# Splitting the exponentials of a float32 attention product into two float32r halves

## The chip, the cores and the metric

The kernel runs on one core of one Trainium2 chip. The metric is the device time of one execution in microseconds; several executions are made and their median is quoted. The kernel before took 4827.44 us (median of 3 runs, 4765.34 to 4841.02). The runs of the kernel before scatter by 1.6%, and with their clock: 4765 us goes with a mean granted clock of 0.955, 4840 us with 0.930. "Faster" and "slower" are verdicts at 2%; a ratio whose interval lies across that mark is called unclear.

## The reference

Two attention layers over an image batch of 8 x 512 x 32 x 32. Layer 0 has 8 heads of 64 channels and quantises q, k and v to 8 bits ("fake quantisation"), so that they are integers times a scale. Layer 1 is one full-width attention and is not touched here.

```python
# layer 0, cut
h = group_norm(xf, gn_w, gn_b)
qkv = einsum('oc,bct->bot', qkv_w, h) + qkv_b[None, :, None]
q, k, v = split(qkv.reshape(b * 8, -1, T), 3, axis=1)      # T = 1024
q, k, v = fake_quant(q), fake_quant(k), fake_quant(v)      # (integer) * scale
w = einsum('bct,bcs->bts', q * scale, k * scale)
w = softmax(w, axis=-1)
a = einsum('bts,bcs->bct', w, v)                           # <- the product that changes
a = einsum('oc,bct->bot', proj_w, a) + proj_b
x = xf + a
```

## The kernel before

Each head takes eight steps, one per tile of 128 key tokens. A step computes the scores of those keys against all 1024 queries (`st`), takes their exponential (`pt`), and adds the product of the exponentials with the integer values (`av`). The row maxima that the *next* head needs are computed in between: scores the other way round (`sm`), reduced on VectorE (`negm`). The integers of q and k are held as bfloat16, in 64 rows; three more rows carry minus the row's maximum, in three bfloat16 parts.

```python
ps_s = tc.tile_pool(name="ps_s", bufs=2, space=PSUM)    # two slots, shared by st and sm
q_aug = [augp.tile([AUG, T], BF, ...) for i in range(2)]   # AUG = 64 + 3 rows
k_aug = [augp.tile([AUG, T], BF, ...) for i in range(2)]

def row_max(g, t):
    ps = big_ps(f"sm_{g}_{t}")
    for hf in range(NH):                                # two halves of 512 tokens
        nc.tensor.matmul(ps[:, bass.ts(hf, 512)],
            lhsT=q_aug[a][0:CH, bass.ts(t, P)], rhs=k_aug[a][0:CH, bass.ts(hf, 512)], ...)
    nc.vector.tensor_reduce(negm[g][:, t : t + 1], ps, AX.X, ALU.max, negate=True)
# [cut]
def step_av(s):
    pt = pts.pop(s)
    for hf in range(NH):
        nc.tensor.matmul(av[hf][0 : CH + 1, :], lhsT=vq[b][:, s, h, :],
            rhs=pt[:, bass.ts(hf, 512)], start=(s == 0), stop=(s == NT - 1))

for s in range(NT):
    ps = big_ps(f"st_{g}_{s}")
    for hf in range(NH):
        nc.tensor.matmul(ps[:, bass.ts(hf, 512)],
            lhsT=k_aug[a][:, bass.ts(s, P)], rhs=q_aug[a][:, bass.ts(hf, 512)], ...)
    pts[s] = ptp.tile([P, T], F32, tag="p", ...)
    nc.scalar.activation(pts[s], ps, AF.Exp, scale=esc)
    if nxt is not None:
        row_max(nxt, s)
    if s > 0:
        step_av(s - 1)
step_av(NT - 1)
if nxt is not None:
    put_max(nxt)                                        # maxima into rows 64:67 of q_aug
# [cut: sums, reciprocal, output]
```

## Time and profile before

| | before |
|---|---|
| median time | 4827.44 us |
| TensorE / VectorE / ScalarE busy | 93% / 37% / 23% |
| attention of layer 0, one image | 240.7 us |
| one steady step of a head | 2.79 us |
| one head, not the first of an image (mean) | 30.75 us |

The prediction below shows the busy times, the chain, the groups and the step. Three further lines of the kernel before matter for what follows. From its page: the row of the granted TensorE clock over 40 equal slices, in tenths of full speed, and the group of the score product (count, busy us and mean ns of one, idle time before and what ended it).

```profile
PEclk9999998999988998899889998999899988998899
...
L357 PE MATMUL st<-q_aug,k_aug 67*128 67x512 bf16 x1024 | 350.6, 418 | 53.5 <-DVE q_aug L312 44.0
```

The attention of image 6 as a stretch (busy time and instruction count of TensorE, its weight loads, VectorE, ScalarE and GpSimd, then granted clock, DMA share, GB/s).

```profile
3314.15:3554.90 240.75, 217.62 (x576) 57.11 (x575) 116.41 (x155) 95.48 (x93) 9.08 (x7) 0.86 0.09 29
```

The clock is at 0.9 or 0.8 nearly everywhere. Inside attention it averages 0.86: it drops at each change of heads, when TensorE waits, and is back after 3.4 us in the shortest heads (28.2 us) and after up to 17.1 us in the longest (34.1 us).

### The profile page before, as it was taken

Reading aid. Unit: us, or ns where it says so; the run is one execution under the profiler, and the core shown is the slowest. Engines: PE = TensorE matmul, PEld = TensorE weight load, DVE = VectorE, ACT = ScalarE, POOL = GpSimd, SP = SyncE. Lnnn points to the kernel's source line nnn. Section 1 sums busy time; section 2 is a strip of 40 time slices with the busy share of each in tenths; the row PEclk is TensorE's granted clock in tenths of the full one; section 3 lists DMA queues with packets and bytes.
Section 4 is the critical chain, followed back from the end, with each engine's and each line's share of the span. In section 5 each row is a group of like instructions: output and inputs, shape, how many; then the busy total and the mean of one; then the engine's idle time right before and its main releaser. Section 6 shows DMA issues by size and latency. Waiting matters only on the chain.

```text
span 4828.6 us, 28560 instructions
## 1 busy us (share of the span) xinstructions
PE 4482.2 (93%) x11328; PEld 1704.1 (35%) x11328; DVE 1781.7 (37%) x2618; ACT 1120.7 (23%) x1217; POOL 108.8 (2%) x102
## 2 busy tenths in 40 slices
PE   7999897889988998999989999999999988998999
PEld 3444442234322442244224422343234322442244
DVE  4544445541245114511442234323442245124311
ACT  0000002421243114311341133213321233124211
POOL 0000000000000000000000000000000000000000
PEclk9999998999988998899889998999899988998899
DMA  4222212010101000100100000001000101000000
GB/s 178 96 90 89 79 74 87 18 31 0 40 18 31 0 35 18 31 4 9 40 18 22 9 35 18 27 0 44 18 27 0 40 18 31 0 35 14 1 0 18
DMA packets 69830, 162.31 MB, mean 34 GB/s; under 512 B 23232, under 2 KB 23232, under 8 KB 69056
## 3 DMA queue, kind: packets, MB, share of 16 engines
q1 hardware_dynamic: 64176, 135.31, 8.0%
q10 hardware_dynamic: 5520, 25.17, 1.4%
q8 instruction: 89, 1.46, 0.1%
q14 instruction: 45, 0.37, 0.0%
HBM read 92.82 MB, written 67.11 MB: 33 GB/s over the span
## 4 chain that ended last, share of the span: by engine, by line
PE 85%; DVE 7%; issue 3%; ACT 2%; DMA 2%; POOL 0%; SPq 0%; POOLq 0%; ACTq 0%; DVEq 0%
PE av L346 19%; PE qk L417 9%; PE o L478 9%; PE s L444 9%; PE pj L394 9%; PE qkps L172 8%; PE sm L285 6%; PE st L357 5%; PE v2ps L431 5%; PE vps L190 4%; DVE negm L292 3%; PE tp L470 1%; DVE q_aug L312 1%; DMA x<-in_x_dram 1%; ACT pt L365 1%
## 5 line engine op out<-in xcount | busy, mean ns | idle before, releaser
L346 PE MATMUL av<-pt,vq 128*65 128x512 f32 x2048 | 1126.9, 678 | 70.6 <-ACT pt L365 70.6
L292 DVE TENSOR_REDUCE negm<-sm 128x1 f32<-128x1024 f32 x512 | 626.0, 1224 | 891.9 <-PE sm L285 891.1
L365 ACT ACTIVATE pt<-st,esc 128x1024 f32<-128x1024 f32 x512 | 569.9, 1113 | 1003.2 <-PE st L357 1003.2
L346 PEld LDWEIGHTS av<-pt,vq 128*65 128x65 f32 x2048 | 298.9, 152 | 602.0 <-issue 420.2
L172 PE MATMUL qkps<-h,wqkv 128*128 128x512 f32 x1024 | 462.4, 615 | 30.7 <-ACT h L123 30.4
L417 PE MATMUL qk<-h,wres 128*128 128x512 f32 x1024 | 457.8, 610 | 29.6 <-ACT h L123 29.6
L444 PE MATMUL s<-k,q 128*128 128x512 f32 x1024 | 443.4, 592 | 0.0
L478 PE MATMUL o<-pT,v 128*128 128x512 f32 x1024 | 442.9, 593 | 0.3 <-DVE pT L472 0.3
L285 PE MATMUL sm<-k_aug,q_aug 64*128 64x512 bf16 x1024 | 348.1, 424 | 59.3 <-DVE negm L292 32.3
L357 PE MATMUL st<-q_aug,k_aug 67*128 67x512 bf16 x1024 | 350.6, 418 | 53.5 <-DVE q_aug L312 44.0
L402 DVE SCALAR_TENSOR_TENSOR x<-pj,vec,x 128x512 f32<-128x512 f32 x128 | 95.3, 750 | 643.3 <-PE pj L394 641.6
L172 PEld LDWEIGHTS qkps<-h,wqkv 128*128 128x128 f32 x1024 | 201.6, 198 | 285.6 <-issue 252.8
L417 PEld LDWEIGHTS qk<-h,wres 128*128 128x128 f32 x1024 | 200.4, 197 | 281.1 <-issue 250.8
L478 PEld LDWEIGHTS o<-pT,v 128*128 128x128 f32 x1024 | 193.9, 190 | 244.5 <-issue 241.1
L438 DVE TENSOR_TENSOR v<-v2ps,vb 128x512 f32<-128x512 f32 x64 | 44.2, 691 | 632.2 <-PE v2ps L431 632.2
L444 PEld LDWEIGHTS s<-k,q 128*128 128x128 f32 x1024 | 193.3, 190 | 237.2 <-issue 237.2
L285 PEld LDWEIGHTS <-q_aug 64*128 64x128 bf16 x1024 | 64.7, 96 | 523.2 <-issue 427.2
L123 ACT ACTIVATE h<-h,vec 128x1024 f32<-128x1024 f32 x64 | 68.3, 1137 | 750.7 <-DVE h L119 750.7
L394 PE MATMUL pj<-q,wres 128*128 128x512 f32 x512 | 222.3, 592 | 0.0
L394 PE MATMUL pj<-ao,wres 128*128 128x512 f32 x512 | 221.8, 594 | 0.0
L431 PE MATMUL v2ps<-wres,h 128*128 128x512 f32 x512 | 221.0, 592 | 0.0
L190 PE MATMUL vps<-wqkv,h 128*128 128x512 f32 x512 | 221.0, 592 | 0.0
(108 smaller groups left out, 2315.3 us busy)
## 6 DMA issues: line engine op xcount, KB each, us to landing
qk_d<-qk SPq DMA_DIRECT2D x64, 512.0 KB, 2.6
rqk<-qk_d SPq DMA_DIRECT2D x64, 512.0 KB, 3.7
x<-in_x_dram SPq DMA_DIRECT2D x32, 512.0 KB, 6.3
v_d<-v SPq DMA_DIRECT2D x64, 256.0 KB, 2.0
x<-in_x_dram ACTq DMA_DIRECT2D x8, 2048.0 KB, 7.9
rv<-v_d SPq DMA_DIRECT2D x32, 512.0 KB, 4.2
out_dram<-x SPq DMA_DIRECT2D x16, 1024.0 KB, 4.2
wres<-in_w_res_dram ACTq DMA_DIRECT2D x5, 1024.0 KB, 9.7
```

The source lines that it names most:

```text
L172: nc.tensor.matmul(ps[:, bass.ts(hf, 512)], lhsT=wqkv[:, cc, h * 3 * CH : h * 3 * CH + 2 * CH], rhs=hn[:, cc, bass.ts(hf, 512)], start=(cc ...
L190: nc.tensor.matmul(ps, lhsT=hn[:, cc, bass.ts(t, P)], rhs=wv_cols[:, cc, :, 2, :], start=(cc == 0), stop=(cc == CC - 1),)
L285: nc.tensor.matmul(ps[:, bass.ts(hf, 512)], lhsT=q_aug[a][0:CH, bass.ts(t, P)], rhs=k_aug[a][0:CH, bass.ts(hf, 512)], start=True, stop=True,)
L292: nc.vector.tensor_reduce(negm[g][:, t : t + 1], ps, AX.X, ALU.max, negate=True)
L346: nc.tensor.matmul(av[hf][0 : CH + 1, :], lhsT=vq[b][:, s, h, :], rhs=pt[:, bass.ts(hf, 512)], start=(s == 0), stop=(s == NT - 1),)
L357: nc.tensor.matmul(ps[:, bass.ts(hf, 512)], lhsT=k_aug[a][:, bass.ts(s, P)], rhs=q_aug[a][:, bass.ts(hf, 512)], start=True, stop=True,)
L365: nc.scalar.activation(pts[s], ps, AF.Exp, scale=esc)
L394: nc.tensor.matmul(ps, lhsT=wres[:, w, cc, bass.ts(oc, P)], rhs=src[:, cc, :], start=(cc == 0), stop=(cc == CC - 1),)
L417: nc.tensor.matmul(ps[:, bass.ts(hf, 512)], lhsT=wres[:, w, cc, bass.ts(oc, P)], rhs=hn[:, cc, bass.ts(hf, 512)], start=(cc == 0), stop=(c ...
L431: nc.tensor.matmul(ps, lhsT=hn[:, cc, bass.ts(t, P)], rhs=wres[:, WV1, cc, :], start=(cc == 0), stop=(cc == CC - 1),)
L444: nc.tensor.matmul(ps[:, bass.ts(hf, 512)], lhsT=qt[:, cc, bass.ts(n, P)], rhs=kt[:, cc, bass.ts(hf, 512)], start=(cc == 0), stop=(cc == C ...
L478: nc.tensor.matmul(ps, lhsT=vt[:, m, bass.ts(dc, P)], rhs=pT[:, m, :], start=(m == 0), stop=(m == NT - 1),)
```

## The change

One float32 product is replaced by two cheaper ones. The exponential is taken once into float32 and once into a float32r tile (`hi`; float32r is a four-byte type, as the diff shows where it reads such tiles as float32, and the change assumes that it keeps fewer bits than float32); VectorE computes what is missing (`lo = pt - hi`); and the values, being integers, go into a float32r tile too. In the kernel before a float32 product of 512 columns takes 858 ns (64 instructions, two a product, in 27.47 us) and a bfloat16 product about 0.22 us (`st`, 0.45 us for two): four passes against one, as passes are counted here. Each half should take one pass too; this was my estimate, as the kernel before has no float32r product. The intent is to halve the `av` work, at the price of a second exponential and a subtraction on engines that were under 40% busy. Comments were dropped from the file as well, which changes nothing.

```diff
+F32R = mybir.dt.float32r
+    php = ctx.enter_context(tc.tile_pool(name="php", bufs=2))
-        vq[b] = act.tile([P, NT, HEADS, CH + 1], F32, tag="v", name=f"vq_{b}")
-        nc.gpsimd.memset(vq[b][:, :, :, CH : CH + 1], 1.0)
+        vq[b] = act.tile([P, NT, HEADS, CH + 1], F32R, tag="v", name=f"vq_{b}")
+        nc.gpsimd.memset(vq[b][:, :, :, CH : CH + 1].bitcast(F32), 1.0)
         ...
         def step_av(s):
-            pt = pts.pop(s)
-            for hf in range(NH):
-                nc.tensor.matmul(... rhs=pt[:, bass.ts(hf, 512)],
-                    start=(s == 0), stop=(s == NT - 1))
+            for part, pt in enumerate(pts.pop(s)):
+                for hf in range(NH):
+                    nc.tensor.matmul(... rhs=pt[:, bass.ts(hf, 512)],
+                        start=(s == 0 and part == 0), stop=(s == NT - 1 and part == 1))
         ...
-            pts[s] = ptp.tile([P, T], F32, tag="p", name=f"pt_{g}_{s}")
-            nc.scalar.activation(pts[s], ps, AF.Exp, scale=esc)
+            pt = ptp.tile([P, T], F32, tag="p", name=f"pt_{g}_{s}")
+            nc.scalar.activation(pt, ps, AF.Exp, scale=esc)
+            hi = php.tile([P, T], F32R, tag="hi", name=f"hi_{g}_{s}")
+            nc.scalar.activation(hi, ps, AF.Exp, scale=esc)
+            lo = php.tile([P, T], F32R, tag="lo", name=f"lo_{g}_{s}")
+            nc.vector.tensor_sub(lo, pt, hi.bitcast(F32))
+            pts[s] = (hi, lo)
```

More of the change, by code (lines that the diff above doesn't have):

```diff
@@ L343, in step_av @@
         def step_av(s):
-            pt = pts.pop(s)
-            for hf in range(NH):
-                nc.tensor.matmul(
-                    av[hf][0 : CH + 1, :],
-                    lhsT=vq[b][:, s, h, :],
-                    rhs=pt[:, bass.ts(hf, 512)],
-                    start=(s == 0),
-                    stop=(s == NT - 1),
-                )
+            for part, pt in enumerate(pts.pop(s)):
+                for hf in range(NH):
+                    nc.tensor.matmul(
+                        av[hf][0 : CH + 1, :],
+                        lhsT=vq[b][:, s, h, :],
+                        rhs=pt[:, bass.ts(hf, 512)],
+                        start=(s == 0 and part == 0),
+                        stop=(s == NT - 1 and part == 1),
+                    )
         for s in range(NT):
```

## The prediction

> **What bounds the kernel now.** I read the page's busy times, the chain of waits by line, the groups, and then the timeline of one head in image 6. The page first: TensorE is busy 93% of the span, VectorE 37%, ScalarE 23%, and the chain that ends last is mostly TensorE, with the changed line (L346, `av`) as its largest part.
>
> ```profile
> PE 4482.2 (93%) x11328; PEld 1704.1 (35%) x11328; DVE 1781.7 (37%) x2618; ACT 1120.7 (23%) x1217; POOL 108.8 (2%) x102
> ...
> PE av L346 19%; PE qk L417 9%; PE o L478 9%; PE s L444 9%; PE pj L394 9%; PE qkps L172 8%; PE sm L285 6%; PE st L357 5%; PE v2ps L431 5%; PE vps L190 4%; DVE negm L292 3%; PE tp L470 1%; DVE q_aug L312 1%; DMA x<-in_x_dram 1%; ACT pt L365 1%
> ...
> L346 PE MATMUL av<-pt,vq 128*65 128x512 f32 x2048 | 1126.9, 678 | 70.6 <-ACT pt L365 70.6
> L292 DVE TENSOR_REDUCE negm<-sm 128x1 f32<-128x1024 f32 x512 | 626.0, 1224 | 891.9 <-PE sm L285 891.1
> L365 ACT ACTIVATE pt<-st,esc 128x1024 f32<-128x1024 f32 x512 | 569.9, 1113 | 1003.2 <-PE st L357 1003.2
> ```
>
> The kernel issues 1024 `av` products and the group counts 2048, so one float32 product is two instructions. A busy mean of 678 ns is not the pace, because ends are modelled: the chain has a float32 group of the same moving width with nothing between, 64 instructions in 27.47 us, so 429 ns each and 858 ns a product.
>
> ```profile
> 1148.48 27.47 PE s L444 x64
> ```
>
> Averages hide that the change touches attention of layer 0 only: from 3314.15 to 3554.88 us in image 6, 240.7 us, or 1926 us in eight images, 40% of the span. One steady step there (of eight per head):
>
> ```profile
> 3384.23 0.60 PE L285 MATMUL sm<-k_aug,q_aug 64*128 64x512 bf16 x2
> ...
> 3384.76 0.61 PE L357 MATMUL st<-q_aug,k_aug 67*128 67x512 bf16 x2
> 3384.87 1.23 DVE L292 TENSOR_REDUCE negm<-sm 128x1 f32<-128x1024 f32 x1 [1.66 <-PE sm L285]
> ...
> 3385.21 1.88 PE L346 MATMUL av<-pt,vq 128*65 128x512 f32 x4
> ...
> 3385.47 1.11 ACT L365 ACTIVATE pt<-st,esc 128x1024 f32<-128x1024 f32 x1 [1.68 <-PE st L357]
> ...
> 3387.02 0.60 PE L285 MATMUL sm<-k_aug,q_aug 64*128 64x512 bf16 x2
> ```
>
> Starts give the pace: `sm` 0.53, `st` 0.45, four `av` 1.81, together 2.79 us, with no gap on TensorE. VectorE and ScalarE each idle over 1.5 us of it. So a step is bound by TensorE. A head is not: mrow to mrow is 31.19 us (3398.35 to 3429.54), of which eight steps are 22.3. The rest is the change of heads:
>
> ```profile
> 3399.52 0.38 PE L357 MATMUL st<-q_aug,k_aug 67*128 67x512 bf16 x1 [0.56 <-DVE q_aug L312]
> ...
> 3400.59 1.11 ACT L365 ACTIVATE pt<-st,esc 128x1024 f32<-128x1024 f32 x1 [2.12 <-PE st L357]
> ...
> 3401.76 2.89 PE L346 MATMUL av<-pt,vq 128*65 128x512 f32 x4 [1.26 <-ACT pt L365]
> ...
> 3402.45 1.15 ACT L277 ACTIVATE q_aug<-qi,nmagic 64x1024 bf16<-64x1024 f32 x1 [0.74 <-DVE qi L266]
> ...
> 3404.82 1.01 PE L285 MATMUL sm<-k_aug,q_aug 64*128 64x512 bf16 x2 [0.17 <-ACT k_aug L278]
> ...
> 3406.89 1.11 ACT L365 ACTIVATE pt<-st,esc 128x1024 f32<-128x1024 f32 x1 [2.12 <-PE st L357]
> ```
>
> TensorE waits there for row maxima, exponentials and quantised q and k in turn, and afterwards runs at half clock, as the stretches show (busy times, then the granted clock in the third column from the end):
>
> ```profile
> 3384.00:3395.00 11.00, 11.00 (x33) 3.09 (x32) 4.90 (x4) 4.45 (x4) 0.00 (x0) 1.00 0.00 0
> ...
> 3402.00:3408.00 6.00, 5.49 (x10) 0.90 (x8) 2.55 (x3) 3.40 (x3) 1.30 (x1) 0.55 0.28 88
> ```
>
> [...]858 ns against about 0.22 us for a bfloat16 product (`st`, 0.45 for two).[...] The trace's nearest, L387 on 64 partitions, is 1213.
>
> **The change part by part.** *Removed from TensorE:* per step, four `av` instructions of 429 ns become two products in each of two halves, four instructions again, at one pass each. Taking the bfloat16 pace of 216 ns (my choice; no float32r is in this trace), 2048 x 213 ns = 436 us go. TensorE's step becomes 0.53 + 0.45 + 4 x 0.216 + 0.1 for switches = 1.94 us.
>
> *Added to ScalarE:* a second exponential of the same scores per step, 512 x 1.113 = 570 us. It also keeps the scores' PSUM slot longer.
>
> *Added to VectorE:* 512 subtractions of 128 x 1024 fp32 at about 1.22 us, 625 us. A step has 2.44 us of VectorE work with the maximum; a head 8 x 2.44 + some 5.5 us of small work = 25 us.
>
> *Moved:* `vq` is written as float32r, same instructions; `lo` must wait for both exponentials and for VectorE.
>
> So no engine alone is a bound above 2.79: TensorE 1.94, [...]VectorE 2.44. The path of waits is. A scores slot is held from the start of `st` (0.71 to the first exponential, as above: 3384.76 to 3385.47), through two exponentials (2.25), to release (0.06 seen between an activation's end and its waiter): 3.02 us, against 1.88 now. There are two slots for `st` and `sm` together, and `sm` holds one for 0.64 + 1.23 + 0.06 = 1.93. If `st` keeps coming back to its own slot, **a step takes 3.02 us**, slower than 2.79 although TensorE idles a third of it.
>
> Head: from the last exponential of a head to the second of the next is 13.05 us now (3393.84 to 3406.89), through `av`, copies, sums, then qi, q_aug, k_aug, `sm`, `st`. New: `av` ends later by the second exponential and the subtraction but is shorter by 1.1; I add 1.0 for VectorE's queue: 14.0. Six more steps: 18.1. Half-clock steps at about 3.5 cost 1.3 more. Sum 33.4 against 31.19, **+2.2 us**, for 56 heads +123 us; the first heads of images (23.4 us, few waits now) get 8 x 0.23 plus the longer tail, 3 us each, +24. Sum **+150 us**. Layer 1 and phase 1 don't move.
>
> **Rivals.** *A, TensorE still sets the pace:* then 436 us would go, 4390 us. For it: 93% busy, the chain 85% TensorE. Against: it needs steps of 1.94, below VectorE's 2.44. I give it next to nothing. *B, slots are traded:* `st` can take the slot that `sm` left. One line shows that it happens (a score product waiting for the row maximum just before it):
>
> ```profile
> 3324.44 0.59 PE L357 MATMUL st<-q_aug,k_aug 67*128 67x512 bf16 x2 [1.31 <-DVE negm L292]
> ```
>
> Then the bound is (3.02 + 1.93)/2 = 2.47, near VectorE's 2.44; really some 2.7, as subtractions delay maxima. That takes 0.3 x 6 x 64 = 115 us off: about 4860 to 4880, within 2%. *C, in-order queues lock:* TensorE runs `sm` before `av`, VectorE the subtraction before the maximum. Then two steps take 0.71 + 2.31 + 1.22 + 1.22 (maximum) + 0.12 + 0.53 + 0.97 = 7.0, or 3.5 a step, +185 us on top, about 5160. Now the trace has `st`, `av`, `sm`, which speaks against it. *D, the clock:* at 64% busy TensorE may stay at half rate; steps then take about 3.5, like C. Against: at half rate it would be nearly always busy[...].
>
> **Range and chances.** 4827 + 150 = 4977 by the middle path. C or D at about a third adds 60, B at a fourth takes 30: 5010, and as orders seldom come out ideal I say 5020 us. Range 4870 (B) to 5270 (C and D partly together). Runs of before scatter by 1.6%. Slower by over 2% (above 4924) 0.73, within 2% 0.21, faster 0.06: that needs steps under 2.5 and shorter changes of heads.
>
> **What would show it.** Right: `av` spaced 216 ns; PE busy down by over 400 us while the span grows; exponentials x1024 of 1.11 us; subtractions x512 near 1.22; steady steps at 3.0; `st` waiting for the second exponential; heads at 33 to 34 us; layer 1 unchanged at 264 us an image. Wrong: steps below 2.7 with `st` waiting for maxima (B), 3.5 (C), a low clock in steady steps (D), or a float32r product at more than one pass, which up to two passes would hardly change the time, since TensorE would still be under 2.9 a step.

## The result, and the profile after

The changed kernel took **5203.65 us** (median of 4 runs, 5201.69 to 5206.18), against 4833.65 us for the kernel before in the same session: a ratio of 1.0825, 95% interval 1.0724 to 1.0927. Ratios here and below are the mean time of one kernel's fast runs over that of the other's fast runs of the same rounds, so they are not quite the ratios of the medians.

So the change makes the kernel 8.25% slower, where the forecast of 5020 us meant 4%. The time lies inside the range, but for a reason that the prediction argued against: its middle path was 4977 us, and the room above came from rivals C and D, at about a third together. First the page of the changed kernel: busy times and the clock row, then groups.

```profile
PE 4629.4 (89%) x11328; PEld 1794.2 (35%) x11328; DVE 2391.4 (46%) x3130; ACT 1629.6 (31%) x1729; POOL 126.6 (2%) x102
...
PEclk9999985579856995699559965798569956995699
...
L370 ACT ACTIVATE pt<-st,esc 128x1024 f32<-128x1024 f32 x512 | 570.9, 1115 | 793.0 <-PE st L359 793.0
L348 PE MATMUL av<-hi,vq 128*65 128x512 f32 x1024 | 576.3, 660 | 127.8 <-ACT hi L372 127.8
...
L374 DVE TENSOR_TENSOR lo<-pt,hi 128x1024 fp32r<-128x1024 f32 x512 | 625.6, 1222 | 45.0 <-ACT hi L372 44.3
L359 PE MATMUL st<-q_aug,k_aug 67*128 67x512 bf16 x1024 | 497.6, 575 | 111.9 <-ACT hi L372 63.7
L372 ACT ACTIVATE hi<-st,esc 128x1024 fp32r<-128x1024 f32 x512 | 567.1, 1108 | 0.0
```

The added work costs just what was forecast: 512 more exponentials of 1108 ns, 512 subtractions of 1222 ns. But TensorE's busy time went *up* by 147 us although half its `av` work is gone. The untouched group `st` shows why: 418 ns an instruction before, 575 ns now. The clock row says the same: 5 and 6 stand where 8 and 9 stood. Attention of image 7 (the stretch before was of image 6; images 2 to 7 take the same 240.7 or 240.8 us there), after two parts of it, as stretches:

```profile
4111.80:4134.00 22.20, 17.77 (x70) 6.23 (x70) 19.66 (x22) 15.69 (x16) 0.00 (x0) 1.00 0.38 142
4150.00:4160.00 10.00, 10.00 (x22) 2.75 (x21) 6.76 (x7) 5.86 (x6) 0.00 (x0) 0.50 0.00 0
4111.80:4396.20 284.40, 233.16 (x575) 67.82 (x574) 190.77 (x218) 157.75 (x156) 11.59 (x7) 0.58 0.07 24
```

Attention of an image takes 284.4 us where it took 240.7, at a mean clock of 0.58 instead of 0.86. The image period grew from 505.2 to 549.6 us (553 in some images); 44.4 us by eight images is 355 of the 370 us. Layer 1 and the first phase did not move. The second line is the one to stop at: **TensorE busy for 10.00 of 10.00 us, and still at half clock**. The first head (first line) runs at full clock and has gaps. The timeline of image 7 shows both kinds of step. First head, full clock (start, duration, engine, what ended the gap before it):

```profile
4120.52 0.59 PE L359 MATMUL st<-q_aug,k_aug 67*128 67x512 bf16 x2 [0.47 <-DVE negm L294]
...
4123.32 0.59 PE L359 MATMUL st<-q_aug,k_aug 67*128 67x512 bf16 x2 [0.61 <-ACT hi L372]
...
4125.77 0.59 PE L359 MATMUL st<-q_aug,k_aug 67*128 67x512 bf16 x2 [0.25 <-DVE negm L294]
```

The score product waits by turns for the row maximum and for the second exponential: the two PSUM slots are traded between `st` and `sm`. From 4112.24 to 4128.56 six steps pass, 2.72 us each. All later heads, from the third step on, look like this:

```profile
4198.14 1.08 PE L359 MATMUL st<-q_aug,k_aug 67*128 67x512 bf16 x2
...
4199.15 1.03 PE L287 MATMUL sm<-k_aug,q_aug 64*128 64x512 bf16 x2
4199.25 1.11 ACT L370 ACTIVATE pt<-st,esc 128x1024 f32<-128x1024 f32 x1 [1.62 <-PE st L359]
...
4200.11 1.11 PE L348 MATMUL av<-hi,vq 128*65 128x512 f32 x2
...
4200.26 1.11 ACT L372 ACTIVATE hi<-st,esc 128x1024 fp32r<-128x1024 f32 x1
...
4201.02 1.05 PE L348 MATMUL av<-lo,vq 128*65 128x512 f32 x2
...
4201.88 1.08 PE L359 MATMUL st<-q_aug,k_aug 67*128 67x512 bf16 x2
```

Starts give 1.01, 0.96, 0.91 and 0.86 us for the four pairs, together **3.74 us**, with no gap. Every pair takes near 0.9 us, half the pace of the first head, where `st` took 0.53. All heads but the first of an image take 37.5 us on average, against 30.75 before.

The clock is lost where heads change, as before, when TensorE waits for the exponential and the quantised keys:

```profile
4137.59 1.12 PE L348 MATMUL av<-hi,vq 128*65 128x512 f32 x2 [2.21 <-ACT hi L372]
...
4141.92 1.01 PE L287 MATMUL sm<-k_aug,q_aug 64*128 64x512 bf16 x2 [1.96 <-ACT k_aug L280]
```

What is new is that it does not come back for the steps of the head. It does come back once, at the head's end, where the `av` products of the last two steps stand in a row (eight from 4166.71 to 4170.37 us); but then TensorE waits, and after 3.4 us the clock is lost again. As stretches:

```profile
4136.00:4169.80 33.80, 28.79 (x61) 8.07 (x62) 22.56 (x25) 18.66 (x18) 1.88 (x1) 0.50 0.04 16
4170.00:4173.20 3.20, 1.73 (x12) 0.61 (x10) 1.39 (x3) 1.72 (x3) 0.00 (x0) 1.00 0.02 1
4173.50:4207.30 33.80, 29.16 (x62) 8.21 (x62) 22.73 (x25) 18.30 (x18) 1.82 (x1) 0.50 0.05 16
```

Nearly every head of this run has 34.1 us at half clock and 3.4 us at full. Two questions follow. What is the change worth without the lost clock? And why does a fully busy TensorE stay at half clock?

### The profile page after: what moved, and what is told of

Same layout as the page of the kernel before. It is cut to its first block, busy times and chain, and to the rows that moved or that the text cites. A ratio compares the mean times of both kernels' runs of the same rounds, so it can differ in the third digit from the quotient of the medians.

```text
span 5200.0 us, 29095 instructions
## 1 busy us (share of the span) xinstructions
PE 4629.4 (89%) x11328; PEld 1794.2 (35%) x11328; DVE 2391.4 (46%) x3130; ACT 1629.6 (31%) x1729; POOL 126.6 (2%) x102
## 4 chain that ended last, share of the span: by engine, by line
PE 77%; DVE 9%; ACT 8%; issue 3%; DMA 1%; POOL 0%; SPq 0%; POOLq 0%; ACTq 0%; DVEq 0%
PE av L348 11%; PE qk L427 9%; PE o L488 8%; PE s L454 8%; PE st L359 8%; PE pj L404 8%; PE sm L287 7%; PE qkps L173 7%; PE v2ps L441 4%; PE vps L191 4%; DVE lo L374 3%; ACT pt L370 3%; ACT hi L372 3%; DVE negm L294 2%; DVE q_aug L314 1%
## 5 line engine op out<-in xcount | busy, mean ns | idle before, releaser
L370 ACT ACTIVATE pt<-st,esc 128x1024 f32<-128x1024 f32 x512 | 570.9, 1115 | 793.0 <-PE st L359 793.0
L348 PE MATMUL av<-hi,vq 128*65 128x512 f32 x1024 | 576.3, 660 | 127.8 <-ACT hi L372 127.8
L287 PE MATMUL sm<-k_aug,q_aug 64*128 64x512 bf16 x1024 | 500.8, 589 | 170.7 <-ACT k_aug L280 150.0
L374 DVE TENSOR_TENSOR lo<-pt,hi 128x1024 fp32r<-128x1024 f32 x512 | 625.6, 1222 | 45.0 <-ACT hi L372 44.3
L359 PE MATMUL st<-q_aug,k_aug 67*128 67x512 bf16 x1024 | 497.6, 575 | 111.9 <-ACT hi L372 63.7
L372 ACT ACTIVATE hi<-st,esc 128x1024 fp32r<-128x1024 f32 x512 | 567.1, 1108 | 0.0
L348 PE MATMUL av<-lo,vq 128*65 128x512 f32 x1024 | 514.6, 600 | 21.0 <-DVE lo L374 6.4
L348 PEld LDWEIGHTS av<-hi,vq 128*65 128x65 f32 x1024 | 174.0, 207 | 465.0 <-issue 267.9
L348 PEld LDWEIGHTS av<-lo,vq 128*65 128x65 f32 x1024 | 182.0, 205 | 312.6 <-issue 183.7
```

The lines of the kernel that those rows point to most:

```text
L287: nc.tensor.matmul(ps[:, bass.ts(hf, 512)], lhsT=q_aug[a][0:CH, bass.ts(t, P)], rhs=k_aug[a][0:CH, bass.ts(hf, 512)], start=True, stop=True,)
L359: nc.tensor.matmul(ps[:, bass.ts(hf, 512)], lhsT=k_aug[a][:, bass.ts(s, P)], rhs=q_aug[a][:, bass.ts(hf, 512)], start=True, stop=True,)
L370: nc.scalar.activation(pt, ps, AF.Exp, scale=esc)
L372: nc.scalar.activation(hi, ps, AF.Exp, scale=esc)
L374: nc.vector.tensor_sub(lo, pt, hi.bitcast(F32))
```

## The experiments

There are fourteen runs, in four sessions, each with its own runs of the kernel before on the same chip (medians 4814.75, 4779.62, 4771.87 and 4780.77 us). All gave correct results. "Heads" are the means over the stretches from one `mrow` to the next within an image: all heads but the first of an image (only that of image 1 is among them). "Clock" is the mean granted clock of the whole run: 0.80 for the changed kernel, 0.93 to 0.955 for the kernel before. Where an expectation speaks of the clock in attention (0.58 and 0.86), that of image 7 is given too.

### First: is it the lost clock, and what do the waits cost alone?

The theory at this point was: the idle time at the change of heads starts the half clock, and half-clock steps have too little in them to end it. Rival: the waits (two exponentials per slot, the subtraction) cost the time whatever the clock is.

**e4_f32_extra** leaves the float32 product as it was and adds the second exponential and the subtraction, whose results nobody uses:

```diff
 nc.scalar.activation(pts[s], ps, AF.Exp, scale=esc)
+hi = php.tile([P, T], F32R, tag="hi", ...)
+nc.scalar.activation(hi, ps, AF.Exp, scale=esc)
+lo = php.tile([P, T], F32R, tag="lo", ...)
+nc.vector.tensor_sub(lo, pts[s], hi.bitcast(F32))
```

> The kernel before with only the added ScalarE and VectorE work of the change (second exponential, subtraction, their results not used) and the old float32 product. T: TensorE streams as before, the clock in attention stays near 0.86, steps near 2.8-2.9 us, time 4830 to 4950 us. W: the added work and the slot hold are the cost, so most of the loss is here: time near 5150-5200 us.

Measured: 4971.35 us, ratio 1.0352 (1.028 to 1.0423), clock 0.938, heads 32.92 us. Steps are 2.83 us where TensorE sets the pace and 3.35 where a wait gets in. The added waits cost 157 us by the medians and leave the clock alone (0.89 in attention). The time is just above what T gave and far below W. The prediction's sum for the waits was 150.

**e3_hi_only** takes away the low half, the float32 exponential and the subtraction; its probabilities have only the high half's bits:

```diff
-pt = ptp.tile(...); nc.scalar.activation(pt, ps, AF.Exp, scale=esc)
 hi = php.tile(...); nc.scalar.activation(hi, ps, AF.Exp, scale=esc)
-lo = php.tile(...); nc.vector.tensor_sub(lo, pt, hi.bitcast(F32))
-pts[s] = (hi, lo)
+pts[s] = (hi,)
```

> The changed kernel with the high half alone: one exponential written as float32r, no subtraction, two single-pass products per step[...]. ScalarE, VectorE and slot hold are as before the change, TensorE has far less work. T: TensorE has even less to do, the clock falls at the change of heads and stays at half; a step is then 1.01 + 0.96 + 0.91 = 2.9 us at half clock, a head about 31 us, and the time about 4830 us, no gain. W: with the waits undone, steps are near 1.95 us, a head some 25 us, the time about 4500 us.

Measured: 4735.23 us, ratio 0.9861 (0.9779 to 0.9942; unclear at 2%), clock 0.799 (0.52 in attention), heads 29.2 us. The time lies between the two forecasts, the heads and the clock are near T. With a quarter of the passes of the kernel before left in `av`, and no added waits, it is merely 1.4% faster: the commonest step is 2.79 us again, at half clock. The page's clock row is as low as that of the changed kernel:

```profile
PEclk9999997569955995599658975798569956995699
```

So the half clock comes with the smaller product, not with the added waits.

**e1_warm** fills the idle time at each change of heads of the changed kernel with 20 products whose result is not used:

```diff
+def warm(n, rhs):
+    wt = bank(f"warm_{g}_{n}")
+    for i in range(n):
+        nc.tensor.matmul(wt[0 : CH + 1, :], lhsT=vq[b][:, i % NT, h, :], rhs=rhs, start=True, stop=True)
 ...
+if s == 0: warm(8, <512 columns of vq>); p0 = hi
 # after step_av(s - 1):
+if s == 1: warm(12, p0[:, 0:512])
```

> The changed kernel plus 20 idle-filling TensorE products per head (results never read) around the change of heads; the order of all other TensorE instructions is the same. Theory T (clock): the clock is lost at the change of heads and, at half clock, TensorE itself is the bound with 3.74 us a step, so it never comes back in time. Then granted clock in attention of an image rises from 0.58 to over 0.9, steps fall from 3.74 to about 2.7 us, a head from 37.5 to 31-32 us, and the time to about 4850 us. Rival W (waits): the second exponential, the subtraction and the longer hold of the PSUM slots set the pace and the low clock only follows from TensorE's waiting; then the clock may rise, but the time stays within 2% of 5200 us.

Measured: 5213.14 us, ratio 1.0856 (1.0781 to 1.0932), clock 0.858 (0.71 in attention). A miss: the clock held through the change of heads, but fell two or three steps later (near 4156.5 us in image 7), where TensorE waits for maxima and exponentials, and the rest of the head ran in steps of 3.74 us. Filling one hole is not enough.

**e2_before_warm** is its control, 6 float32 fillers per head in the kernel before, at the same two places.

> Control: the kernel before with 6 float32 idle-filling products per head in the same place. Before has 0.86 clock in attention, and its heads take 28.5 us where the clock stays full and up to 34 us where it drops. T: clock near 1, heads near 28.5 us, 56 heads x 2.4 us = some 135 us less, about 4700 us. W: the clock costs nothing that matters, time within 1% of 4830 us.

Measured: 4840.67 us, ratio 1.008 (1.001 to 1.015), clock 0.982 (1.00 in attention), heads 30.2 us. T's 4700 us is missed: all heads last 30.2 us, where they lasted from 28.2 to 34.1. So the fillers cost about what the clock saves. That the clock is worth nothing here does not follow; e11 below takes 3.1% off.

### Second: can the clock be kept, and what brings it back?

**e7_warm_more** puts 34 fillers per head into the first three steps of the changed kernel: 8 and 20 products as above at step 0, then 7 and 3 bfloat16 products (q_aug by k_aug, 64 rows) after the row maxima of steps 1 and 2.

> The changed kernel with 34 instead of 20 idle-filling products per head, reaching through the first three steps of the next head: in e1_warm the clock stayed full through the change of heads, fell in the first steps after it (idle for maxima and the second exponential) and stayed at half, so the heads kept 37.5 us. T (clock): if the clock now holds, steps in mid-head fall from 3.74 to 2.6-2.8 us, heads to 29-32 us and the time to 4780-4900 us. W (waits): steps stay above 3.3 us at full clock too, time above 5100 us. A third outcome, heads unchanged with the clock falling later still, would say that the steady steps themselves can't hold the clock, against the first head of each image, which holds it for 22 us.

Measured: 5028.37 us, ratio 1.05 (1.044 to 1.056), clock 0.974, heads 33.41 us, fillers' cost included. Now the clock holds, and 3.25 points of the 8.25 are back; the time lies between T's range and W's. That supports the lost clock as a large part of the loss, but fillers stand in the way of real work.

**e8_bf16_halves** changes the data type of `hi`, `lo` and `vq` from float32r to bfloat16, to see whether float32r as such fails to count as activity.

```diff
-vq ... F32R    -hi ... F32R    -lo ... F32R
+vq ... BF      +hi ... BF      +lo ... BF
```

> The changed kernel with the halves and v in bfloat16[...]: the same numbers of instructions on every engine, only the type of av differs. If float32r itself keeps the clock down, the clock comes back: above 0.8 in attention, time below 5000 us. If it is the amount of TensorE work per step, nothing changes: 0.58 and 5200 us within 1.5%.

Measured: 5196.49 us, ratio 1.0849 (1.0797 to 1.0901), clock 0.798, heads 37.38 us. The clock in attention is 0.58, as in the changed kernel, and the half-clock step is 3.66 us against 3.74: the type hardly matters to the speed of the products, and not to the clock.

**e5_av_pairs** runs the `av` products of two steps together, eight in a row, to see whether a long run of full-height products brings the clock back.

```diff
-if s > 0: step_av(s - 1)
+if s % 2 == 0 and s > 0:
+    with tc.issue_after(st_last.ins):
+        step_av(s - 2); step_av(s - 1)
 ...
+step_av(NT - 2)
 step_av(NT - 1)      # php: 3 buffers instead of 2, raw: 2 instead of 3
```

> The changed kernel with the products of two steps issued together, eight av in a row (3.42 us at half clock) in place of four; the same instructions otherwise, one raw buffer fewer and one hi/lo buffer more to hold the parts. It asks what brings the clock back. If it takes an unbroken stretch as long as the four float32 av of before (3.4 us at half clock), the clock comes back early in each head: granted clock in attention above 0.8 and time below 5000 us. If it takes something else (rows in use, the data type), the clock stays near 0.58 and the time near 5200 us or a little above.

Measured: 5274.77 us, ratio 1.1013 (1.0959 to 1.1066), clock 0.842 (0.68 in attention, between the forecasts), heads 38.42 us. The delayed products add waits, so the time says nothing of the clock. The trace does: eight `av` products stand in a row from 4209.03 to 4212.47 us, and the score pair after them takes 0.54 us, the full pace (0.53 in the changed kernel's first head), where the first `av` pair took 0.92. Such a row brought the clock back here, and it was lost again at the waits.

**e6_st128** adds zeros. The score product contracts over 128 rows, of which 61 are zero, instead of 67. It computes the same, in the same order of instructions on each engine as in the changed kernel, with the same number of columns streamed.

```diff
-q_aug = [augp.tile([AUG, T], BF, ...)]; k_aug = [augp.tile([AUG, T], BF, ...)]
+q_aug = [augp.tile([P, T], BF, ...)];   k_aug = [augp.tile([P, T], BF, ...)]
+nc.gpsimd.memset(k_aug[i][CH:P, :], 0.0)    # once, before the ones
+nc.gpsimd.memset(q_aug[i][CH:P, :], 0.0)
```

> The changed kernel with st contracting over all 128 rows (rows 67 to 127 are zeros, same duration, same result). If the activity that brings the clock back is counted by rows in use, a half-clock step goes from (0.5 + 0.52 + 2 x 1.0) of its four parts, 0.70 by time, to about 0.82, the same as before's 0.82, and the clock comes back: granted clock in attention above 0.8, time below 5000 us. If rows don't count, nothing changes: 0.58 and 5200 us within 1%.

Measured: **4922.64 us**, ratio 1.0277 (1.0227 to 1.0326), clock 0.905 (0.81 in attention), heads 32.57 us. Some 5.4% of the changed kernel's time is gone, for zeros. The timeline just after a change of heads shows the clock come back:

```profile
3927.69 1.01 PE L361 MATMUL st<-q_aug,k_aug 128*128 128x512 bf16 x2 [0.85 <-ACT hi L374]
...
3931.34 0.60 PE L361 MATMUL st<-q_aug,k_aug 128*128 128x512 bf16 x2
...
3934.16 0.59 PE L361 MATMUL st<-q_aug,k_aug 128*128 128x512 bf16 x2 [0.51 <-ACT hi L374]
```

The second step of the head lasts 3.65 us at half clock, and the next is at full clock with 2.82. Its half-clock step is no shorter than e8's 3.66 us, where the clock stayed away: so it is not that TensorE has fewer gaps. At full clock the gaps return (0.51 us, for the second exponential): there the waits decide, as in the first head of an image.

### Third: more rows everywhere

**e9_all128** has `sm` over 128 rows too (the three rows of maxima must be cleared for it, once per head). **e10_hi_128** is e3 with the same rows, **e11_before_128** the kernel before with the same rows. The edit that all three share, on top of that of e6:

```diff
 # quant_qk
+nc.gpsimd.memset(q_aug[a][CH:AUG, :], 0.0)
 # row_max
-lhsT=q_aug[a][0:CH, bass.ts(t, P)], rhs=k_aug[a][0:CH, bass.ts(hf, 512)],
+lhsT=q_aug[a][:, bass.ts(t, P)],    rhs=k_aug[a][:, bass.ts(hf, 512)],
```

> The changed kernel with both st and sm over 128 rows of zeros-padded operands (the rows of the maxima set to zero for sm). e6_st128, with st alone, brought the clock back two steps after each change of heads and took 278 us off. If rows in use decide, the rest of the clock comes back sooner or is not lost: granted clock above 0.93, and the time at or a little below e6_st128's 4922 us (its two half-clock steps cost about 1 us each per head, so at most 100 us less). What then remains over the kernel before is the cost of the waits (second exponential, subtraction, slots), some 2 us a head, 130 us: 4830 to 4930 us.

> The high half alone[...] with st and sm over 128 rows. e3_hi_only ran at half clock with steps of 2.79 us and heads of 29.3 us. With the clock back, no wait of the change present: steps near 2 us, heads 24 to 26.5 us, time 4430 to 4600 us, a version that beats both kernels. If the clock is not brought back with so little TensorE work (1.5 us of each 2 us step), it stays near 4735 us.

> Control: the kernel before with st and sm over 128 rows. Its own heads vary from 28.3 us (clock kept) to 34 us (clock lost for some 10 us). If rows in use decide, all heads come near 28.5 to 30 us and the time falls by 60 to 130 us, to about 4680 to 4760 us; if not, no difference (4780 to 4840 us).

| | median us | ratio to before (95%) | clock | heads, us |
|---|---|---|---|---|
| e9_all128 | 4884.63 | 1.0216 (1.0148 to 1.0285) | 0.914 | 31.93 |
| e10_hi_128 | 4397.41 | 0.9196 (0.9145 to 0.9246) | 0.929 | 23.87 |
| e11_before_128 | 4633.42 | 0.9687 (0.9634 to 0.974) | 0.961 | 27.36 |

The exact change, with most of its clock returned, is still 2.2% slower than the kernel before (unclear at 2%), and 5.5% slower (1.0216 / 0.9687) than the kernel before with the same rows. Its clock was to be above 0.93 and is 0.914 (0.83 in attention; 12 us of a head are still at half clock). Waits remain: from the last exponential of a head into float32 to the second of the next, e9 takes 14.63 us (3883.63 to 3898.26) where the kernel before took 13.05, part of it at half clock. What e9 would take at full clock throughout is not shown.

Two versions **beat both kernels**: e11, which computes just what the kernel before does and needs no change of the product at all, and e10, which is faster still but gives the probabilities only the bits of the high half (whether that precision is wanted is another question). Both came out below their forecast ranges. In e11 that is not the clock alone. Its step at full clock is 2.58 us, against 2.79 before: with 128 rows in every product, `sm` to `st` takes 0.43 us instead of 0.53. Why is not shown.

```profile
3820.48 0.59 PE L360 MATMUL st<-q_aug,k_aug 128*128 128x512 bf16 x2
...
3823.06 0.59 PE L360 MATMUL st<-q_aug,k_aug 128*128 128x512 bf16 x2
```

Heads with one stretch of 3.4 us at half clock mostly last 27.2 us in e11 and 28.2 to 28.7 us before. That is 1.0 to 1.5 of the 3.4 us that a head gained, so by this estimate roughly a third of e11's gain is the shorter step, and the rest goes with the clock.

In e10 TensorE is no longer the only bound; the chain's largest part by line is now the row maximum on VectorE:

```profile
DVE negm L297 12%; PE qk L426 10%; PE o L487 10%; PE s L453 10%; PE pj L403 10%; PE qkps L173 9%; PE sm L290 6%; PE v2ps L440 5%; PE vps L191 4%; ACT hi L373 2%; DVE q_aug L317 2%; PE st L362 1%; PE tp L479 1%; DVE qi L270 1%
```

### Fourth: is it the rows?

Every edit of the third group also brought larger tiles and zero fills on GpSimd, and all of them had `st` over 128 rows. Three more runs separate these. **e12_sm128** gives the rows to `sm` alone, **e14_zeros_only** keeps tiles and fills of e12 but neither product's rows, **e13_st96** gives `st` 96 rows.

```diff
 # e12, on top of e9                       # e14, on top of e12
-st: k_aug[a][:, ...], q_aug[a][:, ...]    -sm: q_aug[a][:, ...],    k_aug[a][:, ...]
+st: k_aug[a][0:AUG, ..], q_aug[a][0:AUG]  +sm: q_aug[a][0:CH, ...], k_aug[a][0:CH, ...]
 # e13, on top of e6: tiles [96, T] and fills of rows 64:96 instead of [128, T] and 64:128
```

> The changed kernel with only the row-maximum products over 128 rows (64 of them zero), the score products left at 67. If the rows in use decide whether the clock comes back, this does the same as the score products alone over 128 rows did: share of time weighted by rows (4 x 0.427 + 0.854 + 0.854 x 67/128) / 3.74 = 0.80 at half clock, so the clock is back within some steps of a change of heads, mean clock about 0.90, 4900 to 4950 us. If it was something about the score products themselves, nothing changes: 5190 to 5220 us and clock 0.80.

> The changed kernel with the score products over 96 rows instead of 67 or 128. Weighted by rows its half-clock step is (4 x 0.427 + 0.854 x 96/128 + 0.854 x 64/128) / 3.74 = 0.74, between 0.69 (never back) and 0.80 (back). If the threshold lies above 0.74: about 5200 us, clock 0.80. If below: 4920 to 4960 us, clock 0.90. If the effect is graded: some 5050 us. No theory of mine prefers one; I lean to the first, as the low state also holds through stretches with mixed work.

> Control: the changed kernel with the larger tiles and all the added zero fills on GpSimd, but both products at 64 and 67 rows as before. If the rows decide, nothing is gained: 5190 to 5230 us, clock 0.80. If the fills or their waits shift something that keeps the clock, it comes out near 4890 to 4950 us.

| | rows of st, sm | median us | ratio to before (95%) | clock | heads, us |
|---|---|---|---|---|---|
| e14_zeros_only | 67, 64 | 5199.5 | 1.0863 (1.08 to 1.0925) | 0.80 | 37.48 |
| e13_st96 | 96, 64 | 5146.61 | 1.075 (1.0687 to 1.0812) | 0.83 | 36.35 |
| e12_sm128 | 67, 128 | 4900.61 | 1.0239 (1.0168 to 1.031) | 0.90 | 32.14 |

The control e14 gains nothing, so fills and tiles are not the cause. e12 gains the same as e6 from the other product, so it isn't the score product either. **The rows are the cause.** e14 and e12, from the same session, differ by 299 us for 64 rows of zeros in one small product. In e14, fully busy with 67 and 64 rows, the clock stays where it was:

```profile
4150.00:4160.00 10.00, 10.00 (x23) 2.65 (x22) 7.18 (x6) 5.14 (x6) 0.00 (x0) 0.50 0.01 2
```

At 96 rows none of the three forecasts came true: the clock comes back early in some heads and not in others. Most heads take 37.3 to 38.2 us, 31 to 34 us of it at half clock; 15 of 55 take 32.6 to 33.7 us, because the clock comes back in mid-head. Two heads in succession from that run, as stretches, the first with the steps of one head, the other two with the steps of the next head before and after the turn:

```profile
4093.00:4118.00 25.00, 24.68 (x60) 7.40 (x59) 16.77 (x20) 13.69 (x14) 0.00 (x0) 0.52 0.00 1
4128.00:4138.00 10.00, 8.80 (x20) 2.31 (x20) 7.47 (x7) 6.28 (x6) 0.00 (x0) 0.53 0.00 0
4138.00:4151.00 13.00, 10.55 (x41) 3.49 (x40) 12.08 (x15) 8.82 (x10) 0.00 (x0) 1.00 0.00 0
```

A measure that orders these runs, an estimate of mine, is TensorE's time weighted by the share of rows in use, out of the 128 that `av` contracts over. One pass of 512 columns takes 0.427 us at half clock, the commonest time from start to start within an `av` pair of the changed kernel (twice as long as at full clock, where the prediction's float32 group has two passes in 429 ns). A half-clock step of 3.74 us has four full-height passes in `av` and two each in `st` and `sm`. The estimate is then (4 x 0.427 + 0.854 x rows of st / 128 + 0.854 x rows of sm / 128) / 3.74:

| | estimate | clock comes back within a head |
|---|---|---|
| changed kernel, e14 | 0.69 | only at its end |
| e13 | 0.74 | before its end in about one head of four |
| e6, e12 | 0.80 | yes, after about two steps |
| e9 | 0.91 | yes |

(The divisor 3.74 is measured in the changed kernel and holds 0.32 us for the switches between products. In e12 and e9 part of these switches is gone too: e12's half-clock step lasts 3.40 us, which gives 0.88, and e9's at most 3.46, which gives 0.99. The order stays.) The kernel before, with eight passes in `av`, comes by the same working to 4.29 us in use of a step that would be 12 x 0.427 + 0.32 = 5.44 us at half clock, or 0.79 (its trace has 5.34 us: 0.80), and it recovers. This is an ordering, not a rule: that zero rows count as use is shown, but whether the chip weighs rows in just this way, over which window, and where exactly it turns between 0.69 and 0.80, stays open. Eight full-height products in a row bring the clock back even in the changed kernel, at the end of a head (the row starts at 4166.71 us, and its clock record turns to 1.00 at 4169.92, 3.2 us later), and in e5, so the mean of a step does not decide alone. In the clock records of the changed kernel's trace every stretch but the last is a whole multiple of 3.41 us (34.13 and 3.41 us in turn above); the weight at which the clock turns is not worked out here.

## Why the prediction was wrong, point by point

- **What bounded the kernel.** Right: a TensorE-bound step of 2.79 us, and a head longer than eight steps.
- **Costs of the parts.** Right: exponentials 1108 to 1115 ns (forecast 1113), subtractions 1222 (forecast 1220; the nearest VectorE operation in the kernel before, L387 on two tiles of 64 x 1024, took 1213), one pass for a float32r product (at half clock an `hi` or `lo` pair took 0.91 or 0.86 us, a bfloat16 pair of `sm` or `st` 0.96 or 1.01). A pair of `hi` products took 0.52 us at full clock in the first head, over the forecast of 2 x 216 ns (half of the 429 ns of a float32 instruction is 214.5; the two products of a bfloat16 pair mostly start 215 to 227 ns apart in the kernel before). Not right: "PE busy down by over 400 us". It rose by 147, as nearly all products of these steps ran at half clock.
- **The path of waits.** Its sum came out near, its mechanism only in part, so the nearness is partly luck. Waits alone were to cost 150 us; e4, which is not the changed kernel but adds the waits to the old product, shows 157. But "a step takes 3.02 us" did not occur where the clock was full: the slots are traded (rival B), and the step is 2.72 us, as B had it ("really some 2.7"). Two exponentials in a row start 1.01 us apart (4199.25 and 4200.26) at 1.11 us each, so they overlap by 0.10 us; I had laid down 1.125 each, an estimate.
- **First heads.** Wrong in sign: forecast 3 us longer, measured 21.5 us against 23.4. They start at full clock, keep it through their steps, and show what the steps of the change would do if it were kept.
- **Rival C, queues that lock.** Not seen in the changed kernel: the half-clock step has no gap on TensorE and is paced by it. The steps of 3.35 us in e4 come near it.
- **The step that failed** is rival D, put as "at 64% busy TensorE may stay at half rate; steps then take about 3.5, like C. Against: at half rate it would be nearly always busy". The first sentence was right (3.74 us). So was the busy TensorE, but as an objection it failed: TensorE was busy for all of the 10 us shown, at a clock of 0.50. That a busy TensorE gets its clock back was an assumption of mine; no run had tested it. Busy with rows half empty did not bring the clock back here; e12 against e14 shows it (mean clock 0.90 against 0.80, 4900.61 against 5199.5 us). I had counted any instruction on TensorE as activity in full. Nor did losing it take one long unbroken wait: in the kernel before it fell at 3402.6 us after single waits of 0.50, 0.56, 0.23 and 1.26 us (TensorE busy for 1.49 of the 3.30 us from 3399.20).
- **The sum.** A head was to take 33.4 us: 14.0 for the change of heads, 18.1 for six steps and 1.3 for half-clock steps. It takes 37.5. The six steps take 21.8 us, as all of them stay at half clock: 2.4 more than 18.1 and 1.3. The change of heads takes 15.5 us. There the working had slipped: a second exponential, a subtraction and 1.0 for the queue more, and 1.1 less, make 15.3 of 13.05, not 14.0. So 56 heads take 4.1 us each, 230 us, more than forecast; the first heads, 4.9 us each below forecast, take 39 us back.

In short: added waits cost 157 us where the product stays as it was (e4), of a loss of 370 us. The larger part is the clock: giving most of it back by rows alone takes 281 us off (5203.65 to 4922.64, across two sessions) or 299 us (e14 to e12, in one). The two overlap, as at half clock the waits are hidden under TensorE's slower work (the step of 3.74 us has no gap), so they don't add up exactly.

## What to carry to other kernels

When the passes of a matmul are cut in a stage that loses the clock now and then, ask not only whether TensorE stays busy but over how many rows its products contract: look for the granted clock of a gap-free stretch, and if it reads 0.50, try padding short contractions to 128 rows with zeros, which cost no time on TensorE here (from `st` to the next product 0.52 us at full clock in e6, against 0.53 with 67 rows in the changed kernel's first head). That alone took 3.1% off the kernel before, roughly a third of it by shorter steps and not by the clock. And a saving on the bounding engine that is paid for with a longer hold of a shared PSUM slot was worth here only what the next wait left of it: with most of the clock restored, this one was still 2.2% behind the kernel before.
